# Layer 0's output projection turned round: seven block products for out^T, the inverse sums as a row, heads added by accumulating transfers

## The chip, the cores and the metric

The kernel runs on one core of one Trainium2 chip. The core has TensorE (PE, matrix products), VectorE (DVE), ScalarE (ACT), GpSimd (POOL), a sync engine (SP) whose queue issues most transfers, and 16 DMA engines. The metric is the device time of one execution in microseconds (us). A run of the kernel is repeated, and the median is given.

## What is computed

Two layers on `x`, 8 batches of 32 x 32 = 1024 tokens with 256 channels, all in float32. The reference, cut to its operations:

```python
# layer 0: attention with 4 heads of 256 channels each
q, k, v = split(x @ W_qkv)                     # for each head
atten = softmax(q @ k^T * 256**-0.5)           # 1024 x 1024 for each batch and head
x1 = concat_heads(atten @ v) @ W_out + b_out + x

# layer 1: gated attention with 32-channel f and g
f, g, h = x1 @ Wf + bf, x1 @ Wg + bg, x1 @ Wh + bh
out = gamma * (softmax(g @ f^T) @ h) + x1
```

## The kernel before

**Folding.** For each head, `Wqk = Wq Wk^T` and `Wvo = Wv Wout` are made once. Scores are then (x Wqk) x^T, and a head's share of the layer's result is (P x) Wvo, where P is the matrix of exponentials; the division by the row sums of P is done at the end.

**Seven block products.** Queries, scores and the products of P with x are each a 2 x 2 block product by the scheme with seven block multiplications instead of eight (`seven`, line 234). Its three tasks `one`, `two`, `three` hold products 1, 6, 5, then 2, 7, then 4, 3, in three PSUM accumulators called x, y, z. On the way out VectorE or ScalarE adds these: a copy `e` of x, sums `u` and `v`, and four output blocks (line 264; outputs copied by ScalarE at line 276). The scheme wants four sums of blocks of each operand ahead: `sum_a` (S1 to S4) and `sum_b` (T1 to T4), on VectorE.

**Steps.** The work goes in steps: for each batch and head of layer 0, two half steps of 512 query tokens (`blk` 0 and 1), 64 in all. Layer 1 of batch b-1 is put in as two steps after the second head of batch b; that of the second last batch after all four heads of the last one; that of the last batch is the end of the kernel. The loop at line 917 writes the order of TensorE, VectorE and ScalarE by hand: `put(tasks, *places)` gives each task a place number in the step, and tasks are issued by rising place. The order of one engine is the order in which its instructions are written. GpSimd and the DMA queues aren't in the manual schedule.

In a step the three ranks of work are:

- `a`, this step: six pairs of score tasks (`scores`, line 524), with exponentials on ScalarE;
- `one`, the step before: S1 to S4 of its exponentials (line 580); the key sums over tokens that give the softmax sums (`first`, `second`, lines 582 to 602: two additions, a third, an all-reduce over partitions on GpSimd, and two transfers by a DRAM line that turn the row of sums into a column for each 128 tokens); and its products with x (line 608);
- `two`, the step two before: the rest of its products, the reciprocal of its sums (`invert`, line 604) and the projection (line 629).

**Projection before.** For each 128 tokens of the half, two matmuls with the 128 x 128 block of y as the weights and Wvo (256 wide) moving: 8 matmuls of 128 x 128 x 256 a half, in two tasks. Rows of tokens lie on partitions, so the inverse sum of a token is one number for each partition, and one VectorE instruction per 128 tokens multiplies and adds into `rows1` (line 648). `rows1` begins as x + b_out, four 128 x 512 additions a batch on VectorE (line 431).

**To layer 1.** Layer 1 wants x1^T too. 16 transfers of 64 KB per batch move 32 x 32 squares and VectorE transposes them in place (line 385); in the last batch TensorE does it with 16 transposes (line 350). Queries of the next head, their sums (line 512), the sums of x for the next batch's products (lines 405, 421) and the transposes of the next batch's x (line 382) have places in the steps of the batch before.

Of the kernel before, what the change touches and what calls it, by code (L numbers as in the profile page):

```python
# [16 lines left out]
P = 128  # L17
# [3 lines left out]
def kernel(  # L21
# [14 lines left out]
):  # L36

# [111 lines left out]
    bout_sb = const.tile([P, C], F32, tag="bout", name="bout_sb")  # L149
    bfg_sb = const.tile([P, 1], F32, tag="bfg", name="bfg_sb")  # L150
# [7 lines left out]
    def load_rest():  # L158
        with nc.allow_non_contiguous_dma(reason="small bias vectors, loaded once"):
            nc.sync.dma_start(bout_sb, b_out.partition_broadcast(P))  # L160
# [20 lines left out]
    wblocks = {}  # L181
# [52 lines left out]
    def seven(name, width, parts, matmuls, outs, tags, copy, after=None):  # L234
# [7 lines left out]
        def bank(k):  # L242
            banks[k] = tile_of("ps", [P, NB], f"ps{k}_{name}")[:, :width]
# [22 lines left out]
        def one():  # L266
            for k, number in (("x", 1), ("y", 6), ("z", 5)):
                bank(k)
                product(k, number, True)
            nc.scalar.copy(scratch("e"), banks["x"])  # L270
            add(shaped(scratch("u")), "y", sbs["e"])
# [19 lines left out]
    NARROW = dict(e="eh", u="uh", v="w")  # L291

    def fold_weights(h):
# [20 lines left out]
        def multiply(i, what):  # L314
# [13 lines left out]
            if i == 0:  # L328
                t4 = const.tile([P, 4, P], F32, tag=f"wt{h}", name=f"wt{h}")
                sums = [t4[:, k, :] for k in range(4)]  # L330
                blocks = [t[:, c, ts(e, P)] for c in range(CC) for e in range(CC)]
                run(sum_b(sums, *blocks))
                wblocks[h] = b_operands(blocks, sums)

# [22 lines left out]
    def turn_rows(b, src, dst, layer, scratch=None):  # L357

        Q = 32

        def end():
            if b not in dst:
                dst[b] = tile_of("xT", [P, CC, N], f"x{layer}T_{b}")
            return dst[b]

        def flat(t):
            return t.rearrange("p u n -> p (u n)").rearrange("p (s q) -> p s q", q=P)  # L370

        def move(a, c=None):
            to, rows_v = flat(end() if scratch is None else scratch()), flat(src[b])
            if c is not None:
                to, rows_v = to[:, ts(c, NT), :], rows_v[:, c::CC, :]
            for q in range(P // Q):
                nc.sync.dma_start(to[ts(q, Q), :, ts(a, Q)], rows_v[ts(a, Q), :, ts(q, Q)])

        def piece(k, c):
            to = end()[:, c, ts(k, NB)]  # L380
            if scratch is None:
                nc.vector.transpose(to, to)
            else:
                squares = scratch()[:, k, :].rearrange("p (t c q) -> p t c q", c=CC, q=P)
                nc.vector.transpose(to.rearrange("p (t q) -> p t q", q=P), squares[:, :, c, :])

        return (
            [partial(move, a, c) for a in range(P // Q)
             for c in ((None,) if scratch else range(CC))],
            [partial(piece, k, c) for k in range(NBLK) for c in range(CC)],  # L390
        )

# [32 lines left out]
    def residual(b):  # L425


        def piece(i):
            if i == 0:
                rows1[b] = tile_of("rows", [P, NT, C], f"x1_{b}")  # L430
            nc.vector.tensor_tensor(
                rows1[b][:, ts(i, 2), :], rows[b][:, ts(i, 2), :],
                bout_sb.unsqueeze(1).broadcast_to([P, 2, C]), ALU.add,
            )

        return [partial(piece, i) for i in range(NT // 2)]
# [46 lines left out]
    class Layer0:  # L483
        def __init__(self, b, h):
            self.b, self.h, self.name = b, h, f"{b}_{h}"
            self.p, self.y, self.r = {}, {}, {}
            self.products_of, self.pblocks = {}, {}
# [8 lines left out]
        def queries(self):  # L496
# [6 lines left out]
            def after():  # L503
                t = tile_of("qs", [P, 3, NBLK, HB], f"qs_{self.name}")
                q = self.q.rearrange("p c (k e i) -> p c e k i", k=NBLK, e=2)
                blocks = [q[:, c, e] for c in range(CC) for e in range(2)]
                sums = [blocks[1]] + [t[:, k] for k in range(3)]
                self.pieces = sum_b(sums, *blocks)
                self.blocks = b_operands(blocks, sums)

            def piece(k):
                self.pieces[k]()  # L512

# [7 lines left out]
                WIDE, nc.scalar.copy, after,  # L521
            ), [partial(piece, k) for k in range(4)]

        def scores(self, blk):
# [10 lines left out]
            for g in range(0, half, 2):  # L535
# [3 lines left out]
                def after(g=g, out=out):  # L539
# [8 lines left out]
                         self.blocks[number][:, blk, :])  # L548
# [10 lines left out]
        def sums(self, blk):  # L559
# [6 lines left out]
            def start():  # L566
# [4 lines left out]
                s2 = tile_of("s2", [P, half, HB], f"s2_{n}")  # L571
                s3 = tile_of("s3", [P, half, HB], f"s3_{n}")
                sums = [t[:, 1], s2, s3, t[:, 0]]
# [8 lines left out]
            def first():  # L582
                t = made["t"]
                made["m"] = m = tile_of("m0", [P, 2, 2, HB], f"m_{n}")
                tt(m, t[:, :, 0:2, :], t[:, :, 2:4, :], ALU.add)

            def second():
                m = made["m"]
                r = tile_of("rs", [P, 2, HB], f"rs_{n}")
                tt(r, m[:, :, 0, :], m[:, :, 1, :], ALU.add)  # L590
# [13 lines left out]
        def invert(self, blk):  # L604
            n = self.first + blk * HT
            nc.vector.reciprocal(inverse[:, n : n + HT], self.r[blk])
# [22 lines left out]
        def project(self, blk):  # L629

            b = self.b

            def task(t2):
                pm = tile_of("psm", [P, NB], f"po_{self.name}_{blk}_{t2}")
                for j in range(2):
                    for c in range(CC):
                        nc.tensor.matmul(  # L637
                            pm[:, ts(j, C)],
                            lhsT=self.y[blk][:, c, ts(2 * t2 + j, P)],
                            rhs=folded[self.h][1][:, c, :],  # L640
                            start=(c == 0),
                            stop=(c == CC - 1),
                        )
                for j in range(2):
                    ti = 2 * t2 + j
                    n = self.first + blk * HT + ti
                    acc = rows1[b][:, blk * HT + ti, :]
                    nc.vector.scalar_tensor_tensor(  # L648
                        acc, pm[:, ts(j, C)], inverse[:, n : n + 1], acc, ALU.mult, ALU.add
                    )  # L650

            return [partial(task, t2) for t2 in range(HT // 2)]
# [201 lines left out]
    def weave(*lists):  # L854
# [12 lines left out]
        s=2, rows=4, xT=2, v=2, q=2, qs=2, xt=1, ss=1, s2=1, s3=1, m0=1, rs=1, rb=1,  # L867
        y=2, e=2, u=2, w=1, eh=1, uh=1, st=2, r=8, line=4, ps=6, psm=2,
# [14 lines left out]
    for h, tag in ((1, "rows"), (2, "v"), (3, "rows")):  # L883
# [16 lines left out]
    queries, qsums = first.queries()  # L900
# [16 lines left out]
    for i, (a, blk) in enumerate(steps):  # L917
# [13 lines left out]
        if is_l0(two):  # L931
# [3 lines left out]
            put(u.project(k), *((3, 7) if l0 else (2, 6) if blk == 0 else (3, 7)))  # L935
        if is_l0(one):
# [3 lines left out]
            put(sums[:2] + sums[3:], *((2.2, 3.2, 4.2) if l0 else (0.8, 2.2, 4.5)))  # L940
            put(sums[2:3], 5.2 if l0 else 5.5)
# [11 lines left out]

        if is_l0(nxt) and blk == NBLK - 1:
# [178 lines left out]
```

## Time and profile before

| | |
|---|---|
| time, median of 3 runs | 2338.16 us (2338.06 to 2339.18) |
| profiled execution | 2338.61 us |
| its span | 2336.7 us |
| granted TensorE clock | 0.999 of full speed |

| group | instructions | busy us | ns of one |
|---|---|---|---|
| TensorE, score products (psx, psy, psz of line 247) | 3584 records | | 379 to 380 |
| TensorE, projection (line 637) | 1024 records, two for each matmul | 241.9 | 379 |
| VectorE, residual (line 431) | 32 | 21.2 | 682 |
| VectorE, S1 to S4 (line 580), each | 64 | 77.6 to 77.7 | 1212 to 1214 |
| VectorE, query sums (line 512), 128 x 512 | 128 | 87.9 | 684 to 692 |
| GpSimd, all-reduce (line 593) | 64 | 206.9 | 3233 |

The busy time of a group is the sum over its instructions on one engine. A float32 matmul has two records, so that four matmuls read as "x8". "Idle before" is what the engine waited ahead of a group, with the instruction that ended the wait; idle time of an engine that is not the bottleneck costs nothing. In a timeline the columns are start, length, engine, operation and count.

### The profile page before, as it was taken

The page shows a single profiled execution, that of the slowest core. Times are in us where ns is not written, and L with a number is a line of the kernel's source. Part 1 is how long each engine was busy: PE and PEld are TensorE (multiplying, and loading weights), DVE is VectorE, ACT ScalarE, POOL GpSimd, SP SyncE. Part 2 cuts the span into 40 slices and gives each one's busy share as a digit, 9 for nine tenths or more (in the row PEclk, how much of TensorE's full clock was granted, in tenths as well). Part 3 has the DMA queues.
Part 4 walks back from the last instruction along what each step waited for, and adds up shares of the span by engine and source line. Part 5 has one row for each costly group of instructions (what it writes and reads, how often), then busy time and mean ns, then how long its engine had stood idle before and what let it go on. Part 6 is the DMA issues. An engine that isn't in the chain of part 4 may idle for free.

```text
span 2336.7 us, 26026 instructions
## 1 busy us (share of the span) xinstructions
PE 2326.9 (100%) x10394; PEld 1918.8 (82%) x10394; DVE 1481.7 (63%) x2398; ACT 522.5 (22%) x875; POOL 211.5 (9%) x79
## 2 busy tenths in 40 slices
PE   9999999999999999999999999999999999999999
PEld 7888888788878888788887888878888788888877
DVE  6667775377754767557774577645776457766635
ACT  2222222222221222212222122221222222222222
POOL 0111111011110111101111011110011101101110
PEclk9999999999999999999999999999999999999999
DMA  4000010100101001110011000110001100000100
GB/s 138 1 1 1 1 37 14 34 1 11 27 17 32 1 19 21 19 29 1 19 26 18 24 1 19 30 18 19 1 19 30 19 19 1 1 1 1 30 7 31
DMA packets 170257, 42.94 MB, mean 18 GB/s; under 512 B 158160, under 2 KB 163024, under 8 KB 170128
## 3 DMA queue, kind: packets, MB, share of 16 engines
q1 hardware_dynamic: 170128, 41.20, 8.0%
q8 instruction: 84, 1.38, 0.3%
q14 instruction: 45, 0.37, 0.1%
HBM read 13.37 MB, written 8.52 MB: 9 GB/s over the span
## 4 chain that ended last, share of the span: by engine, by line
PE 99%; DVE 1%; DMA 0%; issue 0%; ACT 0%
PE psy_y L247 14%; PE psy L247 14%; PE psx L247 9%; PE pa_l L834 9%; PE po L637 9%; PE psx_y L247 9%; PE psz_y L247 9%; PE psz L247 9%; PE psy_q L247 4%; PE psx_q L247 2%; PE psz_q L247 2%; PE pr_v_l L466 2%; PE ps_l L746 1%; PE pm_fg L703 1%; PE pwqk L318 0%; PE pwvo L318 0%
## 5 line engine op out<-in xcount | busy, mean ns | idle before, releaser
L593 POOL PARTITION_ALL_REDUCE rb<-rs x64 | 206.9, 3233 | 2046.6 <-DVE rs L591 2019.8
L247 PE MATMUL psx<-q,x0T 128*128 128x256 f32 x1024 | 263.6, 380 | 0.0
L247 PE MATMUL psy<-qs,xs 128*128 128x256 f32 x1024 | 263.0, 379 | 0.0
L247 PE MATMUL psz<-q,xs 128*128 128x256 f32 x1024 | 262.8, 379 | 0.0
L541 ACT ACTIVATE p<-p 128x1024 f32<-128x1024 f32 x128 | 135.3, 1057 | 554.8 <-DVE p L264 554.8
L247 PE MATMUL psy_y<-s,xt 128*128 128x256 f32 x1024 | 242.4, 380 | 0.1
L637 PE MATMUL po<-wvo,y 128*128 128x256 f32 x1024 | 241.9, 379 | 0.0
L247 PE MATMUL psx_y<-p,x 128*128 128x256 f32 x1024 | 241.9, 379 | 0.0
L834 PE MATMUL pa_l<-v_l,s_l 128*128 128x257 f32 x1024 | 232.1, 381 | 0.4 <-DVE v_l L729 0.4
L247 PEld LDWEIGHTS psx<-q,x0T 128*128 128x128 f32 x1024 | 194.0, 190 | 45.2 <-issue 21.0
L637 PEld LDWEIGHTS po<-wvo,y 128*128 128x128 f32 x1024 | 194.6, 190 | 39.5 <-issue 14.8
L834 PEld LDWEIGHTS pa_l<-v_l,s_l 128*128 128x128 f32 x1024 | 193.8, 190 | 36.6 <-issue 10.5
L247 PEld LDWEIGHTS psx_y<-p,x 128*128 128x128 f32 x1024 | 194.7, 190 | 34.0 <-issue 8.6
L247 PEld LDWEIGHTS psy_y<-s,xt 128*128 128x128 f32 x1024 | 191.9, 190 | 30.6 <-issue 2.4
L247 PEld LDWEIGHTS psy<-qs,xs 128*128 128x128 f32 x1024 | 194.5, 190 | 27.0 <-DVE qs L512 0.4
L247 PEld LDWEIGHTS psz<-q,xs 128*128 128x128 f32 x1024 | 194.7, 190 | 26.3
L264 DVE TENSOR_TENSOR u<-psy,e 128x512 f32<-128x512 f32 x128 | 88.4, 691 | 144.3 <-ACT e L270 73.4
L276 ACT ACTIVATE p<-psx 128x512 f32<-128x512 f32 x128 | 76.4, 597 | 413.7 <-PE psx L247 413.6
L264 DVE TENSOR_TENSOR v<-psy,e 128x512 f32<-128x512 f32 x128 | 87.8, 686 | 124.5 <-PE psy L247 124.5
L247 PE MATMUL psy<-qs,x0T 128*128 128x256 f32 x512 | 131.6, 380 | 0.7 <-DVE v L264 0.7
L648 DVE SCALAR_TENSOR_TENSOR x<-po,inverse,x 128x256 f32<-128x256 f32 x256 | 111.9, 478 | 31.3 <-PE po L637 22.4
L270 ACT COPY e<-psx 128x512 f32<-128x512 f32 x128 | 73.8, 576 | 257.8 <-PE psx L247 257.8
(120 smaller groups left out, 2839.8 us busy)
## 6 DMA issues: line engine op xcount, KB each, us to landing
out_dram<-x SPq DMA_DIRECT2D x15, 512.0 KB, 2.6
x<-in_x_dram SPq DMA_DIRECT2D x14, 512.0 KB, 4.6
x0T<-x SPq DMA_DIRECT2D x224, 32.0 KB, 1.9
fg<-x SPq DMA_DIRECT2D x112, 64.0 KB, 2.1
fg<-fg SPq DMA_DIRECT2D x56, 64.0 KB, 2.0
w<-in_L_conv_W_qkv_dram SPq DMA_DIRECT2D x4, 512.0 KB, 7.3
x<-in_x_dram SPq DMA_DIRECT2D x4, 256.0 KB, 4.8
w<-in_L_conv_W_qkv_dram SPq DMA_DIRECT2D x4, 256.0 KB, 6.4
```

What stands on the lines that cost most here:

```text
L247: nc.tensor.matmul(banks[k][:, ts(i, w)], lhsT=lhsT, rhs=rhs, start=first and n == 0, stop=True, skip_group_check=True,)
L264: nc.vector.tensor_tensor(dst, shaped(banks[k]), shaped(other), ALU.add)
L270: nc.scalar.copy(scratch("e"), banks["x"])
L276: copy(outs["11"](), shaped(banks["x"]))
L466: nc.tensor.matmul(pm[:, ts(j, C)], lhsT=src()[:, c, ts(2 * t2 + j, P)], rhs=w()[:, c, :], start=(c == 0), stop=(c == CC - 1),)
L541: exp(both, both)
L593: nc.gpsimd.partition_all_reduce(t, r.rearrange("p e i -> p (e i)"), P, bass_isa.ReduceOp.add)
L637: nc.tensor.matmul(pm[:, ts(j, C)], lhsT=self.y[blk][:, c, ts(2 * t2 + j, P)], rhs=folded[self.h][1][:, c, :], start=(c == 0), stop=(c == ...
L648: nc.vector.scalar_tensor_tensor(acc, pm[:, ts(j, C)], inverse[:, n : n + 1], acc, ALU.mult, ALU.add)
L703: nc.tensor.matmul(pm[ts(k, half)], lhsT=w[:, c, :], rhs=x1T_of[b][:, c, ts(k, NB)], start=(c == 0), stop=(c == CC - 1),)
L746: nc.tensor.matmul(pm, lhsT=self.f[ts(r, CK), ts(j0 + r, P)], rhs=self.g[ts(r, CK), ts(blk, NB)], start=True, stop=True,)
L834: nc.tensor.matmul(pm[:, : C + 1], lhsT=p[:, j, ts(ti, P)], rhs=v[:, j, : C + 1], start=(j == 0), stop=(j == NT - 1),)
```

## The change

In each half step the projection computes out^T = Wvo^T y instead of rows:

- `project` is now a block product in seven matmuls of 128 x 128 x 256, with block sums of Wvo made once per head (`oblocks`, kept in `wo0` to `wo3`) and four sums of the half's y (`yt`, 128 x 256 each, VectorE). The x and y accumulators lie in the two halves of one PSUM bank, z in another (`two_banks`). Five additions and two copies bring out the blocks.
- As tokens now lie along the free axis, the inverse sums are wanted as a row on all partitions: `invert` writes the reciprocals to a DRAM line and reads them back by a broadcast (both on SP). `add` multiplies the 128 x 1024 result by that row on VectorE, and GpSimd issues a 512 KB transfer that adds it into x1^T. Heads are so added by transfers.
- x1^T begins as x^T + b_out: two ScalarE activations of 128 x 1024 a batch (head 0, second half) instead of four VectorE additions.
- Layer 1's rows of x1 come from x1^T: 32 transfers of 32 KB a batch on SP (`turn_back`) and four VectorE transposes. In the last batch the 16 TensorE transposes go, and the same transfers stand at the end of its last step.
- The softmax sums: S2 and S4 share a place, S3 is written over a block of P; the additions over tokens are one reduce of 128 x 2048 instead of a sum of 1024 and one of 512. S4 moves to place 5.6.
- The sums of the queries are made for each half step, four of 128 x 256, those of the second half inside the first half's step, instead of four of 128 x 512 a head.
- Pools: `rows` 4 to 3, `xT` 2 to 3, `s2` and `s3` out, `yt`, `eo`, `uo` in.

The core of the diff:

```diff
         def bank(k):
-            banks[k] = tile_of("ps", [P, NB], f"ps{k}_{name}")[:, :width]
+            if not two_banks:
+                banks[k] = tile_of("ps", [P, NB], f"ps{k}_{name}")[:, :width]
+            elif k == "y":
+                banks[k] = banks["x y"][:, width : 2 * width]
+            else:
+                t = tile_of("psm", [P, NB], f"ps{k}_{name}")
+                banks["x y"], banks[k] = t, t[:, :width]
...
-                product(k, number, True)
+                product(k, number, k != "y" or not two_banks)
...
+    LAST = dict(e="eo", u="uo", v="w")
...
+            else:
+                t4 = const.tile([P, 4, P], F32, tag=f"wo{h}", name=f"wo{h}")
+                sums = [t4[:, k, :] for k in range(4)]
+                blocks = [t[:, c, ts(e, P)] for e in range(CC) for c in range(CC)]
+                run(sum_a(sums, *blocks))
+                oblocks[h] = a_operands(blocks, sums)
...
+    def squares(dst, src, swap):
...
+        def move(a, c):
+            for q in range(P // Q):
+                to, rows_v = dst(), src()
+                if swap:
+                    nc.sync.dma_start(
+                        to[ts(q, Q), :, c, ts(a, Q)], rows_v[ts(a, Q), c, :, ts(q, Q)]
+                    )
...
+        def piece(k):
+            to = dst()
+            n = to.shape[1] * to.shape[2] // 4
+            flat = to.rearrange("p u v i -> p (u v) i")[:, ts(k, n), :]
+            nc.vector.transpose(flat, flat)
...
     def residual(b):
...
-            nc.vector.tensor_tensor(
-                rows1[b][:, ts(i, 2), :], rows[b][:, ts(i, 2), :],
-                bout_sb.unsqueeze(1).broadcast_to([P, 2, C]), ALU.add,
+            nc.scalar.activation(
+                x1T_of[b][:, c, :], xT_of[b][:, c, :], AF.Identity, bias=boutT_sb[:, c : c + 1]
             )
...
-                sums = [t[:, 1], s2, s3, t[:, 0]]
+                sums = [t[:, 1], t[:, 0], blocks[2], t[:, 0]]
...
             def first():
-                t = made["t"]
-                made["m"] = m = tile_of("m0", [P, 2, 2, HB], f"m_{n}")
-                tt(m, t[:, :, 0:2, :], t[:, :, 2:4, :], ALU.add)
+                made["r"] = r = tile_of("rs", [P, 2, HB], f"rs_{n}")
+                nc.vector.tensor_reduce(
+                    r, made["t"].rearrange("p e k i -> p e i k"), op=ALU.add, axis=AX.X
+                )
...
         def invert(self, blk):
+
             n = self.first + blk * HT
-            nc.vector.reciprocal(inverse[:, n : n + HT], self.r[blk])
+            inv = inverse[:, n : n + HT]
+            nc.vector.reciprocal(inv, self.r[blk])
+            line = tile_of("line", [1, NB], f"inv_{self.name}_{blk}")
+            with nc.allow_non_contiguous_dma(reason="columns turn into a row"):
+                nc.sync.dma_start(line.rearrange("o (t p) -> p (o t)", p=P), inv)
+            self.rb[blk] = t = tile_of("rb", [P, NB], f"invb_{self.name}_{blk}")
+            nc.sync.dma_start(t, line[0].partition_broadcast(P))
...
+            def add():
+                o = made["o"]
+                nc.vector.tensor_tensor(
+                    o, o, self.rb[blk].unsqueeze(1).broadcast_to([P, CC, NB]), ALU.mult
+                )
+                nc.gpsimd.dma_start(
+                    x1T_of[self.b][:, :, ts(blk, NB)], o, accum_op=ALU.add
+                )
+
+            return [partial(piece, i) for i in range(4)], seven(
+                f"o_{n}", HB, 1,
+                lambda number: [(0, oblocks[self.h][number], made["b"][number])],
...
-            put(u.project(k), *((3, 7) if l0 else (2, 6) if blk == 0 else (3, 7)))
+            ysums, tasks, add = u.project(k)
+            put(ysums, *((1.6, 1.7, 1.8, 2.1) if l0 else (2.6, 2.7, 2.8, 3.1) if blk == 0 else
+                         (1.1, 1.2, 1.3, 2.1)))
+            put(tasks, *((3, 5.5, 7) if l0 else (5.2, 6, 7.2) if blk == 0 else
+                         (3, 5, 7) if nxt else (2.1, 3, 4.5)))
+            put(add, 7.8 if l0 or nxt and blk == 1 else 7.5 if blk == 0 else 5)
...
-            put(sums[:2] + sums[3:], *((2.2, 3.2, 4.2) if l0 else (0.8, 2.2, 4.5)))
-            put(sums[2:3], 5.2 if l0 else 5.5)
+            put(sums, *((2.2, 3.2, 4.2, 5.6) if l0 else (0.8, 2.2, 3.5, 5.5)))
...
+        if l0 and blk == 0:
+            put(a.query_sums(1), 1.3, 2.3, 3.3, 4.3)
...
-        if l0 and a.h == 0 and blk == 0:
-            put(residual(a.b), 5.3, 6.3, 7.3, 7.4)
+        if l0 and a.h == 0 and blk == 1:
+            put(residual(a.b), 5.3, 7.3)
...
-                moves, turned = turn_rows(a.b - 1, rows1, x1T_of, 1, step(i + 2)[0].fg_tile)
-                put(moves, 0.1, 0.2, 0.3, 0.4)
-                put(turned, 5.4, 6.4, 7.2, 7.4)
+                moves, turned1 = turn_back(a.b - 1)
+                put(moves, *range(1, 9))
             else:
+                put(turned1, 0.4, 2.4, 3.4, 4.4)
...
-            put(transpose_rows(B - 1, rows1, x1T_of, 1), 2.5, 4.5, 8.1, 8.2)
-            put(final.queries(), 2.4, 6.5, 9)
+            put(final.queries(), 2.4, 8.8, 9)
+            moves, turned1 = turn_back(B - 1)
+            put(moves, *[9.1 + 0.1 * k for k in range(8)])
```

## The prediction

> **What bounds the kernel now.** Read first the page's busy shares and its chain of waits.
>
> ```profile
> PE 2326.9 (100%) x10394; PEld 1918.8 (82%) x10394; DVE 1481.7 (63%) x2398; ACT 522.5 (22%) x875; POOL 211.5 (9%) x79
> DVE  6667775377754767557774577645776457766635
> PE 99%; DVE 1%; DMA 0%; issue 0%; ACT 0%
> ```
>
> TensorE is never idle, so a matmul taken away is worth its full time, as long as nothing makes TensorE wait instead. VectorE is 63% busy on average, over 70% in many slices: there the room is small. Second, the waits, then the groups with each shape apart:
>
> ```profile
> PE psy L247 <- DVE v L264: 0.7, 2, 0.3
> POOL rb L593 <- DVE rs L591: 2019.8, 63, 76.3
> ...
> L637 PE MATMUL po<-wvo,y 128*128 128x256 f32 x1024 | 241.9, 379 | 0.0
> L648 DVE SCALAR_TENSOR_TENSOR x<-po,inverse,x 128x256 f32<-128x256 f32 x256 | 111.9, 478 | 31.3 <-PE po L637 22.4
> L585 DVE TENSOR_TENSOR m<-ss 128x1024 f32<-128x1024 f32 x64 | 77.8, 1215 | 0.8 <-DMA fg<-fg 0.7
> L590 DVE TENSOR_TENSOR rs<-m 128x512 f32<-128x512 f32 x64 | 43.5, 680 | 0.0
> L264 DVE TENSOR_TENSOR y<-psz_y,u_y 128x256 f32<-128x256 f32 x64 | 27.2, 424 | 82.0 <-PE psz_y L247 82.0
> L276 ACT COPY y<-psx_y 128x256 f32<-128x256 f32 x64 | 23.8, 372 | 171.2 <-PE psx_y L247 171.2
> L1004 DVE TENSOR_REDUCE counts<-good 128x1 f32<-128x256 f32 x1 | 0.4, 419 | 0.0
> L1004 DVE TENSOR_REDUCE counts<-good 128x1 f32<-128x56 f32 x1 | 0.2, 210 | 0.0
> ```
>
> TensorE waits for VectorE 0.7 us in all; GpSimd has one job of 3.2 us a step. These are durations, one instruction each. The price of a matmul is its spacing, from the full chain:
>
> ```profile
> 116.29 1.73 PE po L637 x8
> ```
>
> Eight records are four matmuls, 0.432 us each. Third, the timeline of one first-half step (starting at 260.23):
>
> ```profile
> 266.27 1.03 PE L247 MATMUL psx<-q,x0T 128*128 128x256 f32 x4
> 266.47 0.42 DVE L264 TENSOR_TENSOR y<-psz_y,u_y 128x256 f32<-128x256 f32 x1 [1.30 <-PE psz_y L247]
> ...
> 271.73 1.22 DVE L580 TENSOR_TENSOR s<-ss,p 128x1024 f32<-128x1024 f32 x1
> 272.86 0.68 DVE L264 TENSOR_TENSOR p<-psy,e 128x512 f32<-128x512 f32 x1
> ...
> 273.17 1.89 PE L247 MATMUL psy_y<-s,xt 128*128 128x256 f32 x8
> ```
>
> and of a later stretch:
>
> ```profile
> 757.02 1.21 DVE L580 TENSOR_TENSOR s<-ss,p 128x1024 f32<-128x1024 f32 x1
> ...
> 758.38 1.97 PE L247 MATMUL psy_y<-s,xt 128*128 128x256 f32 x8
> ```
>
> In the first, S2 (line 580) ends at 272.95 and the matmul that reads it starts at 273.17, 0.22 us behind: S2 comes just in time already. In the second it ends at 758.23 and the matmul starts at 758.38, with 0.15 between. VectorE starts a 1024-element sum every 1.13 us, a 512 every 0.60, a 256 every 0.34, plus 0.12 when it reads its predecessor's result. So the rule used below: a late result costs TensorE its end plus about 0.2 (I take 0.23, the upper end) minus the planned start.
>
> **What the Trainium skill says.** "VectorE: DVE Perf Modes", section "The perf-mode tier table (the rule you actually need)": float32 tensor_tensor runs at 1x, 2293 ns for 2048 elements, and tensor_reduce has only the 1x form. The trace agrees at 1024 (1.21 us). "DMA: Bandwidth & Descriptors", section "SWDGE vs HWDGE vs iDMA": an accumulating transfer can be issued from GpSimd only; section "Anatomy of one DMA — SWDGE (gpsimd) path": about 2.0 us plus bytes/436e3 us. No run shows one yet. "SBUF — State Buffer", section "Who interferes with whom": VectorE with two SBUF inputs contends with GpSimd only where that reads SBUF.
>
> **The change, part by part**, against the profiled run's own 2338.6 us (span 2336.7; 0.45 above the median, so the forecast is lowered by that).
>
> *TensorE.* Projection: 8 matmuls become 7 in each of 64 steps, same size: 64 x 0.432 = -27.7. Sixteen transposes of the last batch go: they take 0.49 + 0.43 + 0.87 = -1.8 in the timeline. Floor 2338.6 - 29.5 = 2309.1.
>
> *VectorE, per step.* Out: four L648 (4 x 0.478 = 1.91), L585 and L590 (1.90). In: nine 256-wide sums (four block sums, five adds, 9 x 0.425 = 3.83), the product with the inverse row (1024 wide, 1.22), one reduce of 2048: the two reduces shown give (419 - 210)/200 = 1.05 ns an element, so 2.15 + 0.15 = 2.3 (both ends: 2.1 and 2.5). Query sums of a half are four of 256, not half of four of 512: +0.3. Together +3.8 us a step; 64 x 3.8 = 246, less the residual, 32 x 0.68 = 22, to ScalarE: VectorE goes to about 73%. By its average it fits. Whether it fits at each place is the question, as the program order is fixed.
>
> *A regular first-half step* (18: heads 1 and 2 of batch 0, heads 0 and 1 of batches 1 to 6, the last batch's four). From the step's start, TensorE's new order is: scores 0-6.04, products 6.04-7.76, projection x, y, z 7.76-9.06, scores 9.06-10.79, value products x 10.79-12.52, then y, which reads S2, planned at 12.70. S1 to S4 are the block sums of the exponentials (line 580), T1 to T4 those of `y` (new), u, v, p22, y12 the sums in PSUM evacuations (line 264). VectorE, by its order and the spacings: y12 6.24, query sum 6.58, T3 6.92, T1 7.26, T2 7.72 to 8.14. The projection's y product wants T2 at 8.19 and gets it at 8.37: 0.18 late. Then v 8.06, p22 8.78, score sum 9.38, S1 9.72, query sum 10.85, reciprocal 11.19, u_o 11.46, S2 11.80 to 13.02; +0.23 is 13.25 against 12.70: 0.55 late. 0.73 x 18 = 13. The bounds: only the first (0.2), and 1.0 if u_o waits for its ScalarE copy.
>
> *First halves of head 3, batches 0 to 6 (7).* The same plus four 512-wide transposes (0.61 each), two of them before S2: +1.2, less what idle gaps of VectorE take up: 1.3 late at S2. Busy sum 26.0 of 27.2 us, so the score sum v is late again at the second group (before, it starts at 796.04 in the timeline and its reader at 799.03, 3.0 us later; +3.8 and a block's worth of query sums less 0.43 of TensorE's time): 1.15. 2.5 x 7 = 17.5 (bounds 1.3 and 3.5).
>
> *Second halves of head 1 before layer 1 (7).* The transposes of x1 move here (0.4 to 4.4), beside reduce and product: 0.9 each, 6.4 (0.3 and 1.3). *Other second halves with queries (19):* reduce and product in a row, 3.4 us against 1.9 before: 0.16, 3 (0 and 0.3).
>
> *Layer-1 first steps (7).* The projection's pieces take both psm banks that layer 1's values use; z waits for the value evacuation, the third values for o21: 0 to 1.1, I take 0.5: 3.5. *The end:* 32 moves of x1 instead of 16 PE transposes; a move took 0.69 us to issue on SP, so 22 us, landing behind the accumulating transfer; the four VectorE transposes then stand ahead of layer 1's values: +2.5 (0 and 5).
>
> *Hidden.* Inverse row: reciprocal at 11.2, column-to-row transfer and broadcast at 2.1 us each behind SP's queue: there by about 18, wanted at 23.3; behind the product stands everything of VectorE. The sums as columns: all-reduce, row out, columns back, as now (line 593 at 258.26, line 600 issued at 262.71, 2.1 us to land: 4.6 after the step's start), and up to four of the new moves ahead on SP, 4 x 0.69: 7.4, wanted at 11.2. The 512 KB accumulation: 2.0 + 1.2 = 3.2 us by the page; below that nothing, above, some 20 us until the next half's add, and only the next all-reduce stands behind it on GpSimd. 32 moves of x1 (22 us) land near 30 us, wanted at 30.9: no cover to spare. Residual and copies (2 x 0.37 a step) on ScalarE, 22% busy: nothing. The all-reduce and its releaser shift by less than 1 us of a 20 us slack.
>
> Sum: 2338.6 - 29.5 + 13 + 17.5 + 6.4 + 3 + 3.5 + 2.5 = 2355.0; less 0.45: 2354.6, say **2354**. The saving breaks even at 29.5/64 = 0.46 us of new waits a step.
>
> **The rivals.** *The order absorbs it (faster).* If T2 and S2 find VectorE's idle gaps (1.30 us before the `y` sum above, where the query sum and T3, T1 would have to fit), one mechanism decides: S2's lateness in a first-half step. At 0.2 there, 1.0 in head 3, 2 for the moved transposes, 1 at the end and nothing else: 3.6 + 7 + 2 + 1 = 13.6, so 2309.1 + 13.6 - 0.45 = 2322. It speaks for it that the product and reduce stand late in a step; against it, that T2 and S2 carry the delay by order, not by chance. It decides below 0.46 a step. *Half of it:* only first halves lose, 13 + 17.5 = 30.5: 2339.2, no change. *The row's transfers become the wait (slower):* if the accumulation holds GpSimd so long that the all-reduce behind it and then the row come late, the product waits with all VectorE behind it: 0.5 us in each of 64 steps adds 32, 2386. GpSimd's 9% speaks against. *It doesn't do what it says:* x and y in one PSUM bank could cost TensorE while ScalarE reads x; TensorE never waited on the two halves of `po` so; 64 x 0.2 = +13, 2367, inside the range.
>
> **How the numbers follow.** A change under 0.2% (4.7 us) can't be told from none: 2333.5 to 2342.8. Chances: my forecast 0.45, with the bank case 0.06; absorbed 0.29; half 0.14; transfers 0.06. The likeliest case's own range, losses 31 to 61, is 2339 to 2370; reaching to the absorbed case and cutting the transfers: 2320 to 2371. Faster 0.31 (absorbed and a little of half), same 0.13, slower 0.56.
>
> **What would show it.** Matmuls named o, y: 7 x 64, chain at 0.432 each. Right, if the waits list PE psy_y for DVE s or PE psy_o for DVE yt with some 10 to 20 us, largest in head 3's first half, and VectorE is at 73%. Wrong, if those rows stay under 10 us (then 2322), or if DVE's product waits for a DMA, or layer 1's steps grow by over 2 us each.

## The result: 205 us slower, and the profile after

The changed kernel takes 2543.36 us (2541.31 to 2549.02 in 4 runs) against 2338.47 us (also 4 runs): a ratio of 1.088, 95% interval 1.0861 to 1.0899. Experiments 8 to 10 have 4 to 12 runs each; the others are single executions, and the four above lie within 0.3% of each other. The forecast was 2354 us with a range of 2320 to 2371. The profiled execution has a span of 2539.2 us at a mean granted TensorE clock of 0.982; before, 2336.7 us at 0.999.

First the page's busy shares, then the waits of TensorE (engine, what waited, for whom; us in total, times, longest):

```profile
PE 2370.1 (93%) x10250; PEld 1905.5 (75%) x10250; DVE 1747.2 (69%) x2834; ACT 586.0 (23%) x1015; POOL 289.2 (11%) x143
```

```profile
PE psy L257 <- DVE v L274: 117.7, 58, 6.2
PE psy L257 <- DVE u L274: 14.5, 7, 2.8
PE psy_y L257 <- DVE ss L612: 7.2, 32, 0.4
PE pm_fg L475 <- DMA x1T<-o: 6.3, 1, 6.3
PE psx_o L257 <- DVE yt L681: 4.2, 8, 0.5
```

TensorE, busy all but throughout before, now stands still 7% of the span. The two waits that the forecast rested on, S2 (`ss`) and T2 (`yt`), are there, but small. What carries the loss is a wait that the forecast had only in head 3: the second score group's `psy` waits for the score sum v, 58 times. (The row for u, 7 times, stands almost wholly in the first half steps behind layer 1.) Why v is late stands in VectorE's groups and in SP's waits:

```profile
L616 DVE TENSOR_REDUCE rs<-ss 128x512 f32<-128x2048 f32 x64 | 237.1, 3704 | 0.0
L690 DVE TENSOR_TENSOR o<-o,invb 128x1024 f32<-128x1024 f32 x64 | 78.2, 1223 | 80.8 <-DMA invb<-inv 80.3
```

```profile
SPq L644 <- DMA inv<-inverse: 510.7, 64, 10.4
```

The reduce takes 3.70 us, not 2.3. The product with the inverse row (line 690) waits 80 us for the row. And SP stands 511 us, 8.0 us a step, before the broadcast (line 644) until the reciprocals have been written to DRAM. In one ordinary first half, which starts at 2150.43 (the timelines of VectorE, SP and TensorE; start, length, engine):

```profile
2171.06 3.71 DVE L616 TENSOR_REDUCE rs<-ss 128x512 f32<-128x2048 f32 x1
...
2175.47 1.23 DVE L690 TENSOR_TENSOR o<-o,invb 128x1024 f32<-128x1024 f32 x1
2176.61 0.68 DVE L274 TENSOR_TENSOR v<-psy,e 128x512 f32<-128x512 f32 x1
```

```profile
2161.93 0.36 SPq L642 DMA_DIRECT2D inv<-inverse  x1
2170.53 0.33 SPq L644 DMA_DIRECT2D invb<-inv  x1
```

```profile
2174.78 1.89 PE L257 MATMUL psy_y<-p,xt 128*128 128x256 f32 x8
2177.35 1.13 PE L257 MATMUL psy<-qs,x0T 128*128 128x256 f32 x4 [0.67 <-DVE v L274]
```

The write of 2 KB is issued at 2161.93 and the broadcast that waits for it at 2170.53. With the broadcast's median landing of 4.8 us (its row is shown below) the row is there at about 2175.3, by estimate: just as VectorE gets through the reduce and the two sums behind it. Both delays end together, and v, in order behind the product, comes too late for TensorE: idle for 0.67 us, and 0.84 us late counted from start to start, as the eight matmul records ahead take 1.73 us. Around layer 1 the product waits for the row itself:

```profile
1648.00 0.41 DVE L274 TENSOR_TENSOR o<-psz_o,u_o 128x256 f32<-128x256 f32 x1
1652.86 1.23 DVE L690 TENSOR_TENSOR o<-o,invb 128x1024 f32<-128x1024 f32 x1 [4.45 <-DMA invb<-inv]
```

```profile
1654.73 2.08 PE L257 MATMUL psy<-qs,x0T 128*128 128x256 f32 x4 [5.91 <-DVE v L274]
```

VectorE is idle 4.45 us before the product, and TensorE 5.91 us before `psy`.

To see where the 202 us of span went, take the start of each half step's first score matmul from the trace, and the length from one such start to the next. In us, for one step of each kind; the last columns are of kernels told of below:

| kind of step | before | changed | sums and 16-byte runs | three places mended | the last kernel |
|---|---|---|---|---|---|
| ordinary first half (batch 7, head 0) | 27.63 | 28.75 | 27.81 | 27.28 | 27.28 |
| ordinary second half (batch 7, head 0) | 33.63 | 35.09 | 33.53 | 33.20 | 33.20 |
| head 3's first half (batch 6) | 27.63 | 30.96 | 29.41 | 28.08 | 27.47 |
| head 1's second half and layer 1 (batch 5) | 83.99 | 92.67 | 85.03 | 84.84 | 83.65 |
| first half behind layer 1 (batch 5) | 25.95 | 30.27 | 25.95 | 25.95 | 25.95 |
| last half and the end | 142.62 | 166.68 | 150.69 | 151.49 | 141.53 |

Summed over batches, 56 us were lost in the six stretches with layer 1, 26 us in the six halves behind them, 24 us in the end and 96 us in all other steps.

### The profile page after: what moved, and what is told of

Same layout as the page of the kernel before. It is cut to its first block, busy times and chain, and to the rows that moved or that the text cites. A ratio compares the mean times of both kernels' runs of the same rounds, so it can differ in the third digit from the quotient of the medians.

```text
span 2539.2 us, 27103 instructions
## 1 busy us (share of the span) xinstructions
PE 2370.1 (93%) x10250; PEld 1905.5 (75%) x10250; DVE 1747.2 (69%) x2834; ACT 586.0 (23%) x1015; POOL 289.2 (11%) x143
## 5 line engine op out<-in xcount | busy, mean ns | idle before, releaser
L693 POOL DMA_DIRECT2D x1T<-o x64 | 78.0, 1219 | 1774.2 <-issue 1160.2
L257 PE MATMUL psz<-q,xs 128*128 128x256 f32 x1024 | 271.8, 389 | 0.0
L257 PE MATMUL psy<-qs,x0T 128*128 128x256 f32 x512 | 145.7, 409 | 117.7 <-DVE v L274 117.7
L887 PE MATMUL pa_l<-v_l,s_l 128*128 128x257 f32 x1024 | 241.8, 393 | 4.0 <-DVE v_l L782 3.3
L257 PE MATMUL psy_y<-p,xt 128*128 128x256 f32 x1024 | 245.0, 383 | 0.0
L616 DVE TENSOR_REDUCE rs<-ss 128x512 f32<-128x2048 f32 x64 | 237.1, 3704 | 0.0
L257 PEld LDWEIGHTS psy_y<-p,xt 128*128 128x128 f32 x1024 | 197.7, 193 | 28.1
L257 PEld LDWEIGHTS psy<-qs,x0T 128*128 128x128 f32 x512 | 96.5, 198 | 154.6 <-DVE v L274 140.8
L690 DVE TENSOR_TENSOR o<-o,invb 128x1024 f32<-128x1024 f32 x64 | 78.2, 1223 | 80.8 <-DMA invb<-inv 80.3
L257 PE MATMUL psy_y<-ss,xt 128*128 128x256 f32 x512 | 123.8, 385 | 7.3 <-DVE ss L612 7.2
```

The lines of the kernel that those rows point to most:

```text
L257: nc.tensor.matmul(banks[k][:, ts(i, w)], lhsT=lhsT, rhs=rhs, start=first and n == 0, stop=True, skip_group_check=True,)
L616: nc.vector.tensor_reduce(r, made["t"].rearrange("p e k i -> p e i k"), op=ALU.add, axis=AX.X)
L690: nc.vector.tensor_tensor(o, o, self.rb[blk].unsqueeze(1).broadcast_to([P, CC, NB]), ALU.mult)
L693: nc.gpsimd.dma_start(x1T_of[self.b][:, :, ts(blk, NB)], o, accum_op=ALU.add)
L887: nc.tensor.matmul(pm[:, : C + 1], lhsT=p[:, j, ts(ti, P)], rhs=v[:, j, : C + 1], start=(j == 0), stop=(j == NT - 1),)
```

## The experiments

Theory A: reduce and row are late together, each costs something, and in ordinary first halves neither gains anything when only it is mended. Theory B: the reduce alone is the cause. Theory C: the row alone is. A fourth suspicion was VectorE's order itself, the forecast's own mechanism.

### 1. Three sums instead of the reduce

```diff
-                nc.vector.tensor_reduce(
-                    r, made["t"].rearrange("p e k i -> p e i k"), op=ALU.add, axis=AX.X
-                )
+                t = made["t"]
+                tt(r, t[:, :, 0, :], t[:, :, 1, :], ALU.add)
+                tt(r, r, t[:, :, 2, :], ALU.add)
+                tt(r, r, t[:, :, 3, :], ALU.add)
```

> The one reduce of 2048 (3.70 us each, 3.63 to the next start) becomes three sums of 128x512 into the same tile (3 x 0.60 + 0.24 = 2.04 us). Theory A (reduce and inverse row end about together, so each alone gives little in first halves): only the second halves gain, 1.5 us in some 25 of them, about 2500 to 2515 us; VectorE's product with the inverse row then waits longer for the row's DMA (more than the 80.3 us of now). Theory B (the reduce alone is the cause): 64 x 1.6 us or more, 2440 us or below. Theory C (the row alone): no change, 2543.

Measured: 2483.56 us, 60 us less than the changed kernel. The ordinary second half falls to the 33.53 us it has with both edits, the ordinary first half (batch 7, head 0) stays late: v came 0.84 us late in it and comes 1.0 us late now. VectorE's wait for the row grows from 80.3 to 116.7 us, as A said. So B is out, and the place where nothing is gained is the one that A named; the gain is larger than A's 28 to 43 us.

### 2. A row that is there already

```diff
-                    o, o, self.rb[blk].unsqueeze(1).broadcast_to([P, CC, NB]), ALU.mult
+                    o8, o8, ones_sb.unsqueeze(1).broadcast_to([P, CC * HT, P]), ALU.mult
```

`ones_sb` holds 1/2048 in every place, `o8` is `o` in pieces of 128.

> The product multiplies by a constant row and waits for no transfer; both transfers of the row are still issued. Left out: the division by the softmax sums. Theory A: the long waits around layer 1 (4.5 and 4.6 us each, 7 times), head 1's first halves (1.8 us, 8 times) and the end (7.5 us) go, ordinary steps stay as they are: about 2465 to 2480 us. Theory B: no change. Theory C: all of it, about 2355 us.

Measured: 2455.4 us, 88 us less; A expected 63 to 78, C 188. The steps behind layer 1 are at 25.95 us again. The ordinary first half of the table keeps its 28.75 us (28.76) and the second its 35.1, as A says.

### 3. Both

The two edits above together.

> Three sums instead of the reduce, and the constant row. Left out: the division by the softmax sums. Theory A: TensorE's wait for v in the second score group is gone, only the S2 and T2 waits and head 3's are left, so 2345 to 2375 us, far below the sum of what the two edits give alone. If the accumulating transfers or the moves on SP are a cause of their own, it stays above 2400.

Measured: 2391.26 us, 152 us less. That is the sum of the two, 148 us, with little over: A's picture of two delays that end together holds in ordinary first halves (27.81 us here, gained by neither alone), but not in the total. And 2391 is above the 2345 to 2375 expected. VectorE's timeline and waits in that kernel show a third loss:

```profile
1528.92 0.69 DVE L275 TENSOR_TENSOR u<-psy,e 128x512 f32<-128x512 f32 x1 [1.25 <-ACT e L281]
1536.84 0.71 DVE L397 STREAM_TRANSPOSE x<-x 128x512 f32<-128x512 f32 x1 [7.23 <-DMA line<-rb]
```

```profile
DVE x L397 <- DMA line<-rb: 35.6, 5, 7.8
DVE x L397 <- DMA x<-x1T: 10.8, 2, 6.9
```

No engine waits for the row any more, but SP still waits for its write: 8 us a step, with x1's 32 moves behind it on the queue. VectorE's transposes of x1 (line 397) then wait up to 7.8 us, 46 us in all, and everything of VectorE waits behind them; TensorE's wait for `yt` goes from 4.2 to 17.0 us. (The first of the two rows names another transfer on the same queue; that the moves are what is late is a reading of it, which the next experiment bears out.)

### 4. The write in runs of 16 bytes

The tokens of a half are given to partitions so that four neighbours lie on one: the write is then 128 runs of 16 bytes, not 512 of 4. The columns of sums are read in the same order, so that read has 16-byte runs too. The three sums are in as well.

```diff
-                    nc.sync.dma_start(st, line.rearrange("o (t p) -> p (o t)", p=P))
+                    nc.sync.dma_start(st, line.rearrange("o (p t) -> p (o t)", p=P))
...
-                nc.sync.dma_start(line.rearrange("o (t p) -> p (o t)", p=P), inv)
+                nc.sync.dma_start(line.rearrange("o (p t) -> p (o t)", p=P), inv)
```

> Three sums, and the inverse sums written with four neighbouring tokens on a partition (128 runs of 16 bytes instead of 512 of 4), the columns read in the same order. If the 8.2 us of the write come from its 512 single elements, it takes about a quarter of what it did above 2 us, the row comes some 4 to 6 us earlier and the time is near that of the two edits together, 2350 to 2385 us. If they come from the round trip by DRAM as such, the time is that of the three sums alone, about 2500 us.

Measured: 2367.82 us, 176 us less than the changed kernel, and 23 us less than with the constant row in experiment 3. These 23 us lie in the six stretches with layer 1 (19.4) and in the end (4.3). SP's timeline in an ordinary first half:

```profile
2013.91 0.32 SPq L643 DMA_DIRECT2D inv<-inverse  x1
2015.89 0.32 SPq L645 DMA_DIRECT2D invb<-inv  x1
```

From write to broadcast it is 1.98 us, in place of 8.6. The least over all steps is 1.4 us, against 8.2 before the edit. So the form of the write was the cause, its many short runs, and not the round trip by DRAM; whether by the number of runs or by their size, which changed together, no run tells. The read of the columns gains less, 1.6 us instead of 2.1. VectorE's waits before x1's transposes fall from 46 to 7.5 us: the queue is free again.

### 5. Only the 16-byte runs

> Only the 16-byte runs; the reduce of 3.70 us stays. The two edits add up so far (60 for the sums, 88 for the free row, 152 both). If they do here too, this is 60 us above the run with both, 2420 to 2440 us. If the reduce matters only while the row is late as well, it is below 2400.

Measured: 2448.8 us. That is 81 us above the kernel with both edits, so here the reduce is worth more than the 60 us it was worth with the slow row: with the row late, part of its gain is hidden. The ordinary first half is at 28.75 us again: neither edit alone gains anything there. The upper end of the expectation was missed by 9 us.

### 6. The reduce measured by itself

Ten reduces of 128 x 2048 were put behind the last product of the changed kernel, two of each form; its time means nothing.

```diff
+    for n, view in enumerate((
+        big.rearrange("p e k i -> p e i k"),
+        flat.rearrange("p (e i k) -> p e i k", e=2, k=4),
+        flat.rearrange("p (k i) -> p i k", k=8),
+        flat.rearrange("p (i k) -> p i k", k=8),
+        flat.rearrange("p (i k) -> p i k", k=1024),
+    )):
```

> The changed kernel with ten reduces of 128x2048 behind its last product, only to measure them: as in the kernel (four elements 1 KB apart for each of 512 results), four neighbours for each of 512, eight 1 KB apart for each of 256, eight neighbours, and 1024 neighbours. If the distance costs, the strided ones take 3.7 us and the others 2.2; if the number of results costs, the first two take 3.7 us, those with 256 results some 2.9 and the last 2.2.

VectorE's groups in five windows, two reduces each (busy us, mean ns of one, idle before); in this order: four elements 1 KB apart, four neighbours, eight 1 KB apart, eight neighbours, 1024 neighbours:

```profile
L1089 DVE TENSOR_REDUCE r<-big 128x512 f32<-128x2048 f32 x2 | 7.2, 3619 | 0.2
L1089 DVE TENSOR_REDUCE r<-big 128x512 f32<-128x2048 f32 x2 | 4.6, 2286 | 0.1
L1089 DVE TENSOR_REDUCE r<-big 128x256 f32<-128x2048 f32 x2 | 7.2, 3591 | 0.1
L1089 DVE TENSOR_REDUCE r<-big 128x256 f32<-128x2048 f32 x2 | 4.6, 2286 | 0.1
L1089 DVE TENSOR_REDUCE r<-big 128x2 f32<-128x2048 f32 x2 | 4.6, 2286 | 0.1
```

Neighbours cost 2.29 us, whatever the number of results: the forecast's 2.3. The distance costs the rest, a factor of 1.58.

### 7. VectorE's order in layer 0

```diff
-            put(add, 7.8 if l0 or nxt and blk == 1 else 7.5 if blk == 0 else 5)
+            put(add, 8.6 if l0 else 7.8 if nxt and blk == 1 else 7.5 if blk == 0 else 5)
...
-            put(a.query_sums(1), 1.3, 2.3, 3.3, 4.3)
+            put(a.query_sums(1), 5.1, 5.2, 5.3, 5.35)
...
-            put(turned, 0.4, 1.4, 3.4, 4.4)
+            put(turned, 0.4, 0.45, 3.4, 4.4)
```

> Sums and 16-byte runs, and three places in layer-0 steps: the query sums of the second half behind u_o's value products (5.1 to 5.35) instead of ahead of T3 and S2, the product with the row at 8.6 behind the score sum v, two transposes of head 3 at once at 0.4. The forecast's mechanism (T2 and S2 late by VectorE's order): TensorE's waits of 0.1 + 0.1 and 0.33 + 0.08 in first halves, 0.34 in second halves and 1.6 more in head 3's go, 0.5 x 24 + 0.34 x 25 + 1.6 x 7 = 32 us, so about 2336 us (2332 to 2345). If VectorE is simply full, the lateness moves elsewhere and the time stays within 10 us of 2368.

Measured: 2346.07 us, 22 us less; 32 were expected. The steps of layer 0 alone gained 24 us. Ordinary halves did what was expected: a second half is 0.43 us shorter than in the kernel before, exactly one matmul, and a first half 0.35. Head 3's first halves gained 9 us instead of 15 in all, and second halves 5 instead of 8.5. The stretches with layer 1 and the end, which were not meant to change, took 3.7 us more.

### 8 to 10. The order around layer 1

First, the projection in layer 1's first step was put at 2.6, 4.5 and 6.9, its sums and its product with the row a little earlier too, with three of layer 1's values behind it; x1's transposes came later, and in the end behind the values.

```diff
-            put(ysums, *((1.6, 1.7, 1.8, 2.1) if l0 else (2.6, 2.7, 2.8, 3.1) if blk == 0 else
-                         (1.1, 1.2, 1.3, 2.1)))
-            put(tasks, *((3, 5.5, 7) if l0 else (5.2, 6, 7.2) if blk == 0 else
+            put(ysums, *((1.6, 1.7, 1.8, 2.1) if l0 else (1.2, 1.3, 1.4, 1.5) if blk == 0 else
+                         (1.1, 1.2, 1.3, 2.1) if nxt else (0.55, 0.6, 0.65, 0.7)))
+            put(tasks, *((3, 5.5, 7) if l0 else (2.6, 4.5, 6.9) if blk == 0 else
...
-            put(add, 8.6 if l0 else 7.8 if nxt and blk == 1 else 7.5 if blk == 0 else 5)
+            put(add, 8.6 if l0 else 7.8 if nxt and blk == 1 else 7.2 if blk == 0 else 5)
...
-                put(turned1, 0.4, 2.4, 3.4, 4.4)
+                put(turned1, 0.4, 4.4, 5.45, 6.4)
...
-            put(a.values(), 0.9, 1, 3, 5, 8)
+            put(a.values(), 0.9, 1, 7.3, 7.4, 8)
...
-    weave((prod[2:] + own[1:], 0, 1), (s1, 0.3, 0.7), (p1[:2], 0.55, 0.95), (p0[2:], 0.1, 0.9), (turned1, 0.3, 1))
-    weave((final.products(0), 0, 1), (p1[2:], 0, 0.9), ([judge, decide], 0.9, 1))
+    weave((prod[2:] + own[1:], 0, 1), (s1, 0.3, 0.7), (p1[:2], 0.55, 0.95), (p0[2:], 0.1, 0.9))
+    weave((turned1, -0.1, 0), (final.products(0), 0, 1), (p1[2:], 0, 0.9), ([judge, decide], 0.9, 1))
```

> The same, and in layer 1's first steps the projection split around the value products (2.6, 4.5, 6.9) with three of layer 1's values behind it; x1's transposes spread later; in the end they stand behind layer 1's values. The psm waits there (1.9 us a batch) and the end's v_l waits (3.4 + 1.2 + 0.6 us) go: another 18 us, about 2318 us (2312 to 2328), faster than the kernel before. If another wait takes their place: 2330 or more.

Measured: 2340.24 us, ratio to the kernel before 1.0007 (0.9999 to 1.0016): no change. The end gained 5.8 us, the stretches with layer 1 nothing. TensorE's waits show why:

```profile
PE psx_o L257 <- DVE v_o L274: 6.9, 8, 0.9
PE psy L257 <- DVE v L274: 4.1, 8, 0.5
PE psx_o L257 <- DVE yt L682: 3.5, 9, 0.4
```

The first and the last row lie in the stretches with layer 1 and in the end: the pieces of the projection now waited for their own sums (`yt`, `v_o`). The middle row lies in head 3's first halves, all but once. So the next kernel put products or scores between the pieces, and moved a sum out of head 3's first half.

```diff
-            put(tasks, *((0.5, 2.4) if blk == 0 else (0.5, 2)))
+            put(tasks, *((0.5, 7.1) if blk == 0 else (0.5, 2) if nxt else (0.5, 2.5)))
...
-            put(ysums, *((1.6, 1.7, 1.8, 2.1) if l0 else (1.2, 1.3, 1.4, 1.5) if blk == 0 else
+            put(ysums, *((1.6, 1.7, 1.8, 2.1) if l0 else (2.3, 2.35, 2.4, 2.45) if blk == 0 else
...
-            put(tasks, *((3, 5.5, 7) if l0 else (2.6, 4.5, 6.9) if blk == 0 else
+            put(tasks, *((3, 5.5, 7) if l0 else (4.2, 7.05, 7.15) if blk == 0 else
...
-            put(key_sums(a.b + 1), 5.4, 6.4, 7.2, 7.4)
+            keys1 = key_sums(a.b + 1)
+            put(keys1[:3], 5.4, 6.4, 7.2)
+        if l0 and a.h == HEADS - 1 and blk == 1 and a.b + 1 < B:
+            put(keys1[3:], 0.4)
...
-                put(turned1, 0.4, 4.4, 5.45, 6.4)
+                pass
...
+            put(turned1, 0.1, 2.46, 4.3, 5.6)
```

> The last kernel, and around layer 1: in its first step the projection's tasks stand behind products, with products and scores between them (4.2, 7.05, 7.15), x1's transposes stand in that step instead of head 1's second half; the fourth key sum goes from head 3's first half to the start of its second; at the end one score task stands between two projection tasks. If these waits (2.85 us more than the seven products save in each of six such stretches, 0.8 in each of seven first halves of head 3, 1.5 at the end) come from the order alone, they go for the most part: 2340 - 20 = 2320 us (2315 to 2330), faster than the kernel before. If layer 1's steps have no room for the projection's waits, it stays at 2335 or above.

Measured: 2329.34 us, ratio 0.9956 (0.994 to 0.9973). The `psx_o` rows are down to 0.2 us; besides the waits at the kernel's start one row of over 1 us is left, S2 in layer 1's first step:

```profile
PE psy_y L257 <- DVE ss L612: 6.7, 7, 1.0
```

S2 stood on VectorE behind a value evacuation and the reciprocal, both of which waited (0.84 us for TensorE, 0.48 us for the column of sums). It was moved up, and the reciprocal and a transpose down:

```diff
-            put([partial(u.invert, k)], 2.9 if l0 or blk == 1 else 1.9)
+            put([partial(u.invert, k)], 2.9 if l0 or blk == 1 else 2.5)
...
-            put(sums, *((2.2, 3.2, 4.2, 5.6) if l0 else (0.8, 2.2, 3.5, 5.5)))
+            put(sums, *((2.2, 3.2, 4.2, 5.6) if l0 else (0.8, 0.85, 3.5, 5.5)))
...
-            put(turned1, 0.1, 2.46, 4.3, 5.6)
+            put(turned1, 2.46, 4.3, 5.6, 5.7)
```

> The kernel before it, with one more place mended: in layer 1's first step S2 stands right behind S1 instead of behind a value evacuation, the reciprocal and a transpose of x1. TensorE's wait for S2 there (1.1 us and 0.1 behind it, 7 times) goes: 2329 - 8 = 2321 us (2318 to 2326). If VectorE is full in that step, the wait moves to another row and the time stays within 3 us of 2329.

Measured: 2320.38 us, ratio 0.9922 (0.9905 to 0.9938): 19 us faster than the kernel before. The busy shares of its page, and TensorE's waits behind the kernel's start, but for one of 0.2 us:

```profile
PE 2306.3 (99%) x10250; PEld 1887.0 (81%) x10250; DVE 1660.5 (72%) x2962; ACT 584.1 (25%) x1015; POOL 284.3 (12%) x143
```

```profile
PE psy L257 <- DVE u L274: 0.8, 5, 0.2
PE pa_l L888 <- DVE v_l L783: 0.4, 1, 0.4
PE psy L257 <- DVE v L274: 0.3, 1, 0.3
PE psx_o L257 <- DVE v_o L274: 0.3, 1, 0.3
```

VectorE does the same work as in experiment 4 (1660.5 us busy against 1648.6), and TensorE hardly waits for it any more, under 2 us in all: it was not full, it was out of order.

### 11 and 12. Each cause put back

> The kernel above with the 4-byte runs back. The row then comes some 7 us later, about 13.5 us after the reciprocal: just in time for the product in ordinary steps (its place is now 1.1 us later), late around layer 1 and in the end: 30 to 70 us more than with the 16-byte runs. If the row's delay were only harmful together with the reduce, it would be under 10 us.

Measured: 2412.25 us, 92 us more, above the 30 to 70 expected; so the row's delay does harm without the reduce too. Ordinary halves keep 27.28 and 33.20 us: there the late row still fits, now that the product stands behind v. The loss is in the stretches with layer 1 (94.49 us for batch 5, 10.8 more) and in the end (156.28 us, 14.8 more). The product waits for the row again:

```profile
DVE o L691 <- DMA invb<-inv: 96.9, 29, 6.7
```

> The kernel above with the strided reduce back, 1.6 us more VectorE time in each of 64 steps. If that lies on the path wherever v waits behind it, 40 to 80 us more (60 were gained when it was taken from the changed kernel); if the mended places leave room for it, under 20.

Measured: 2373.55 us, 53 us more, as expected: the ordinary second half goes to 33.97 us, and TensorE waits for v again:

```profile
PE psy L257 <- DVE v L274: 26.8, 40, 1.5
```

## Why the prediction was wrong

The sign was right and the size was not: 205 us instead of 16. Two terms of the sum were mis-sized, and both stand in the forecast as durations of a few us; a third, TensorE's clock, isn't in the sum.

**"One reduce of 2048 ... 2.3 (both ends: 2.1 and 2.5)" failed.** It is 3.70 us. The rate was taken from two reduces over neighbours, and for neighbours it is right (2.29 us by itself). This one adds elements 1 KB apart. Price: 60 us when it is taken out of the changed kernel, 81 when the row is quick, 53 when it is put back into the last kernel.

**"Hidden. Inverse row: ... column-to-row transfer and broadcast at 2.1 us each ... there by about 18" failed.** The 2.1 us were those of the column's read, 512 elements of 4 bytes from DRAM. The write of the same 512 elements takes 8.2 us at the least. The broadcast takes 4.8:

```profile
invb<-inv SPq DMA_DIRECT2D x64, 256.0 KB, 4.8
x1T<-o POOLq DMA_DIRECT2D x64, 512.0 KB, 5.2
```

So 4.2 us were 13.4: 8.6 from write to broadcast, and 4.8. The row comes at about 24.9 in the ordinary first half shown above, against a product wanted at 23.3. Price: 88 us by making the product free of it (92 with the three sums in), 95 us (2543.36 - 2448.8) by quicker writes, and 116 (2483.56 - 2367.82) with the three sums in, since quicker writes free the queue too. The forecast counted the moves of x1 that stand ahead of the transfer on SP's queue, not those that stand behind SP's wait for it. Its own sign of being wrong, "if DVE's product waits for a DMA", is the row of 80.3 us above.

The rival "the row's transfers become the wait" had this mechanism, but put it on GpSimd's accumulation, and priced it at 0.5 us in each step with a chance of 0.06. The accumulation lands after 5.2 us in the median, not after the 3.2 that the forecast took from the page; ordinary halves reach their gain beside it. TensorE waits for it once, at the end, for 6.3 us (`pm_fg` in the first list); with the quick row that wait is gone, so it came from the late product ahead of the transfer.

**The clock, at nothing in the sum.** Behind its long waits TensorE runs for about 3 us at half its pace (last section). In the changed kernel some 150 matmul records do so behind waits, each starting 0.43 us after the one before instead of 0.22: about 32 us by estimate, a sixth of the loss. The prices above contain it, as it goes with the long waits: with both terms mended (experiment 4) the clock is back at 0.999.

With both terms mended, experiment 4 tests the rest of the sum. It stands at 2367.8 us, against 2354:

- *TensorE: right.* 0.43 us a half step, seen in full in the second halves (33.63 to 33.20).
- *A regular first half, 0.73 us: right in place and nearly in size.* TensorE lost 0.21 at T2 and 0.41 at S2, 0.61 us with rounding (27.81 - 27.63 + 0.43). Experiment 7 moved the query sums from before T2 and S2 and all but 0.08 of it went, so it was VectorE's order, as put.
- *Head 3's first half, 2.5 us: right in size.* It is 2.2 us (29.41 - 27.63 + 0.43): 0.8 at T2, 0.4 at S2 and 1.0 at v, where the forecast had 1.3 at S2 and 1.15 at v.
- *Second halves, 0.16 us: too small.* 0.33 us, from the product ahead of v.
- *Head 1's second half and layer 1, 0.9 + 0.5 us: too small.* 85.03 - 83.99 and three missing matmuls' 1.29 make 2.3 us a batch. TensorE's waits in experiment 4 show S2 (0.44 us each) in head 1's second half, and in layer 1's first step u_o (0.24) and o (0.44), the sums that read the projection's PSUM banks; of these the forecast had named o:

```profile
PE psy_y L257 <- DVE ss L612: 7.3, 32, 0.4
PE pr_v_l L495 <- DVE o L274: 3.1, 7, 0.4
PE psx_o L257 <- DVE u_o L274: 2.4, 8, 0.7
```

- *The end, +2.5 us before savings: far too small.* It is 8.1 us longer than before although TensorE has less to do. TensorE waits for layer 1's values, which stand behind x1's transposes as the forecast had it (3.3 us at the longest; experiment 8, which put the values first, shortened the end by 5.8 us), and at pieces of the projection (0.2 to 0.7 us each), which it had not priced there.

The last kernel comes near the 2322 us of the rival "the order absorbs it", but by another way: the reduce and the write were replaced and the order was written anew. The order of the changed kernel doesn't absorb it.

## What to carry to other kernels

A duration from a row carries over only with its access pattern and its direction: a reduce over neighbours doesn't price one over distant elements, and a read of single elements doesn't price their write. Where a transfer waits for another on one queue, count what stands behind the wait on that queue, and who waits for it. When an engine at 70% makes the bound engine wait, move its instructions by what waits for them before believing that it is full: moved places alone were worth 47 us here (2367.82 to 2320.38).

## What the runs showed of the hardware that was not expected

- *Reduce.* 3.62 us for elements 1 KB apart, 2.29 for neighbours. The Trainium skill, "SBUF — State Buffer", section "Door 1: The DMA port swizzle (why `[64,N]` ≈ `[32,N]`)", says that SBUF has 16-byte lines and that each access to a new line pays. The measured factor of 1.58 agrees with that direction; no run here tried other distances, so the line as the cause is not shown.
- *Single elements to DRAM.* A write of 512 elements of 4 bytes takes 8.2 us at the least from its issue to that of the broadcast that waits for it, one of 128 runs of 16 bytes 1.4. The read of 512 elements takes 2.1 us in the changed kernel, from issue to landing.
- *TensorE's clock after a wait.* The windows around the wait at 1654 (length, busy us and instructions of PE, PEld, DVE, ACT and POOL, granted clock, DMA share, GB/s):

```profile
1640.00:1648.00 8.00, 8.00 (x38) 7.02 (x38) 6.46 (x7) 1.83 (x4) 0.00 (x0) 1.00 0.09 11
1648.00:1654.00 6.00, 0.82 (x4) 0.38 (x2) 1.55 (x4) 0.00 (x0) 0.00 (x0) 0.75 0.26 44
1654.00:1658.00 4.00, 3.27 (x8) 2.66 (x9) 3.15 (x7) 0.43 (x1) 3.31 (x2) 0.52 0.44 77
1658.00:1662.00 4.00, 4.00 (x22) 3.22 (x24) 1.38 (x3) 1.26 (x2) 1.13 (x1) 1.00 0.39 55
```

The timeline of TensorE behind that wait:

```profile
1656.60 1.64 PE L257 MATMUL psz<-q,xs 128*128 128x256 f32 x4
1658.08 1.89 PE L257 MATMUL psy_y<-p,xt 128*128 128x256 f32 x8
1659.81 1.89 PE L257 MATMUL psz_y<-ss,x 128*128 128x256 f32 x8
```

After 5.9 us of idling the granted clock is 0.52 in the window in which work starts again. The eight matmul records from 1654.73 take 3.35 us from start to start, and the eight from 1658.08 take 1.73: that adds 1.6 us to the wait. The Trainium skill, "TensorE: Matmul & The Clock Gate", section "What's actually happening", tells of this: half the clock after some 3.4 us without work, until about as long of work. In the changed kernel's trace such slow stretches stand behind all 8 waits of over 5 us, as the page has it, behind one of 3.3 us, and also behind 10 of the 18 waits of 2.1 to 2.9 us, which are shorter than the page's time; behind the 21 waits of 1.6 to 2.0 us there are none. The mean clocks fit: 0.982 in the changed kernel, 0.999 in the last one, and 1.000 in experiment 12, where TensorE waits 26.8 us for v but never over 1.5 us at once. Long waits cost more than they last.
